# Filtered images stored in the order of the convolution's taps, and a GpSimd copy that restores the order for the queries

## The chip, the cores and the metric

The kernel runs on one core of one Trainium2 chip. The metric is the device time of one execution, in microseconds (us); lower is better.

## The reference, cut to what matters

The input x has 16 images of 64 channels and 128 x 128 pixels, in fp32. Layer 0 shifts each channel by a function of its median, upsamples by two with a 7-tap filter, applies a ReLU and downsamples. Layer 1 filters the result in the frequency domain and then runs attention in which the queries are pixels and the keys come from two strided convolutions:

```
x = layer0(x)                                   # zd in the kernel
xf = x + irfft2(rfft2(x) * gate)                # xfd: the filtered images
q = x_flat(xf) @ q_w + q_b                      # one query a pixel, 4 heads of 16
for stride in (8, 16):                          # two paths
    xs = conv(xf, sr_w, stride) + sr_b          # 64 -> 64 channels, kernel = stride
    kv = layernorm(xs) @ kv_w + kv_b            # 256 and 64 keys
    k, v = split(kv);  v = depthwise3x3(v)
out = softmax(q @ k.T / 4) @ v                  # over the 320 keys of both paths
return (out @ proj_w + proj_b) as image + x
```

## The kernel before, in words

The work has two phases. `phase1` goes over images and groups of four channels. It computes layer 0, the Fourier transform, the gate, and the inverse transform, and stores two sets of images in device memory: zd (layer 0's output) and xfd (the filtered images). The last two steps matter here. `inverse_cols` (L546) multiplies a spectrum, as the stationary operand, with the constants iv1 and iv2 (L86, L87), whose 128 columns for each of the real and imaginary parts are the positions w in an image row. `inverse_rows` (L565) finishes the transform, and GpSimd issues the store to xfd (L576), in runs of one image row of 128 elements. So the order of the columns of iv1 and iv2 is the order in which the pixels of a row lie in xfd.

`phase2` reads them twice. For the convolutions, `load_images` (L678) brings a pair of images into the tile xp: 128 partitions (two row parities x 64 channels), and in each partition 2 images x 64 rows x 128 columns. `keys_values` (from L683) is called 8 times, once for a pair of images, in the middle of the image before the pair (the first time at the start of the phase). For stride 8 it issues 32 matrix products of 512 columns, for stride 16 128 products of 128 columns (L698): each takes the 64 x 128 weights of one pair of taps (row d, column f) and, as the moving operand, every pixel that this tap meets. Two consecutive products write the two halves of the PSUM tile cp (partitions 0 to 63 and 64 to 127), so they use the two groups of 64 columns of the array. In the profile each such product is two records. L706 (VectorE) adds the bias and writes cp to xs; then come the layer norm, the keys, the values and their depthwise convolution.

For the queries, `load_part` (L786) brings one part of an image (512 pixels in each of two image halves, 128 partitions) into a tile xa with three buffers, three parts ahead; `queries` (L794) multiplies it with the query weights into qp, two parts ahead. The attention runs over blocks: 16 images x 16 parts x 2 halves = 512. The list `ORDER` (L925) fixes the order of a block's steps on TensorE: maxima of the scores (ma), scores (ss), values (av), in odd blocks the projection of the part before (pj), in even ones the queries. `ordered` (L777) keeps TensorE's and VectorE's attention instructions in this order; the rest is placed by the scheduler of the language. ScalarE takes the exponential (L862); VectorE takes the maxima (L826) and divides by the sum (L895 to L901).

The SP queue issues the loads (xp, xa, zr) and the small transfers that put the transposed maxima into the query tile (q<-nt, L835). GpSimd's queue holds in this phase the transfers of the result (L913) and, for each call of `keys_values`, four memsets of padded value tiles (L735), which wait until VectorE has read the pads of the call before.

Of the kernel before, what the change touches and what calls it, by code (L numbers as in the profile page):

```python
# [8 lines left out]
F32 = mybir.dt.float32  # L9
# [3 lines left out]
ALU = mybir.AluOpType  # L13
# [52 lines left out]
CST_AT, CST_N = _cols(_CST)  # L66
# [4 lines left out]
def _constants():  # L71

    c = np.zeros((128, CST_N), np.float64)
    i = np.arange(128)
    c[:, CST_AT["ident"]] = np.eye(128)
    c[:, CST_AT["ones"]] = 1.0
    turn = (i[:, None] * i[None, :]) % 128
    cos = np.cos(2 * np.pi * turn / 128)
    sin = np.sin(2 * np.pi * turn / 128)
    cos[turn % 64 == 32] = 0.0  # L80
    sin[turn % 64 == 0] = 0.0
    c[:, CST_AT["fh"]] = np.concatenate([cos[:, :65], -sin[:, 1:64]], 1)
    c[:, CST_AT["fwc"]] = cos / 128
    c[:, CST_AT["fws"]] = sin / 128
    c[:, CST_AT["fwn"]] = -sin / 128
    c[:, CST_AT["iv1"]] = np.concatenate([cos, sin], 1)  # L86
    c[:, CST_AT["iv2"]] = np.concatenate([-sin, cos], 1)  # L87
    fold = np.where((i == 0) | (i == 64), 1.0, 2.0)[:, None] / 128

    ihc, ihs = fold * cos, -fold * sin  # L90
    ihs[0] = ihc[64]
    c[:, CST_AT["ihc"]] = np.concatenate([ihc[:64], ihc[:64]])
    c[:, CST_AT["ihs"]] = np.concatenate([ihs[:64], ihs[:64]])
    c[:, CST_AT["rank"]] = np.arange(16)

    c[:, CST_AT["center"]] = ((i[:, None] % 64) == np.arange(C)[None, :]) - 1.0 / C

    vinit = np.zeros((128, 384), np.float32)
    for h in range(NH):
        for j in range(2):  # L100
            vinit[:, 128 * j + 32 * h + 16 : 128 * j + 32 * h + 32] = 1.0
        r, at = 64 * (h % 2), 256 + 64 * (h // 2) + 32 * (h % 2)
        vinit[r : r + 64, at + 16 : at + 32] = 1.0
    return c.astype(np.float32), vinit
# [518 lines left out]
def phase2(ctx, tc, nc, cs, ident, vinit, w2, sr1, sr2, zd, xfd, out):  # L623

    N = 512
# [4 lines left out]
    io = ctx.enter_context(tc.tile_pool(name="p2io", bufs=3))  # L630
# [23 lines left out]
    def wt(name, rows=64):  # L654
        return w2s[0:rows, W2_AT[name]]
# [27 lines left out]
    def keys_values(b, xp):  # L683

        kgs = [kvp.tile([128, NK], F32, name=f"kg{b + i}", tag="kg", bufs=3) for i in range(2)]

        vts = [ks.tile([64, NK + NK2], F32, name=f"vt{b + i}", tag=f"vt{i}") for i in range(2)]
        for s, wgt, size, cols in (("1", s1, 16, c1), ("2", s2, 8, c2)):
            stride, m = H // size, size * size
            n = f"{b}_{s}"  # L690

            c_ps = misc(f"cp{n}")
            src = xp.rearrange("p i (a d) (e f) -> p i a d e f", d=stride // 2, f=stride)
            taps = [(d, f) for d in range(stride // 2) for f in range(stride)]
            for j in range(0, len(taps), 2):
                for y in range(2):
                    d, f = taps[j + y]
                    nc.tensor.matmul(  # L698
                        c_ps[64 * y : 64 * y + 64, 0 : 2 * m],
                        wgt[:, d, f, :],  # L700
                        src[:, :, :, d, :, f],
                        start=(j == 0),
                        stop=(j + 2 == len(taps)),
                    )
            xs = ks.tile([128, 2 * m], F32, name=f"xs{n}", tag="xs")
            nc.vector.tensor_scalar(xs, c_ps[:, 0 : 2 * m], wt("srb" + s, 128), None, ALU.add)  # L706

            n_ps = misc(f"center{n}")
            nc.tensor.matmul(n_ps[0:64, 0 : 2 * m], cs("center"), xs, start=True, stop=True)
            xc = ks.tile([64, 2 * m], F32, name=f"xc{n}", tag="xc")  # L710
            nc.vector.tensor_copy(xc, n_ps[0:64, 0 : 2 * m])
            sq = ks.tile([64, 2 * m], F32, name=f"sq{n}", tag="sq")
            nc.vector.tensor_tensor(sq, xc, xc, ALU.mult)
            q_ps = misc(f"var{n}")
            nc.tensor.matmul(q_ps[0:64, 0 : 2 * m], cs("ones", 64)[:, 0:64], sq, start=True, stop=True)
            sd = ks.tile([64, 2 * m], F32, name=f"sd{n}", tag="sd")
            nc.scalar.activation(sd, q_ps[0:64, 0 : 2 * m], AF.Sqrt, scale=1.0 / C, bias=eps[0:64])
            nc.vector.reciprocal(sd, sd)
            nc.vector.tensor_tensor(xc, xc, sd, ALU.mult)
            yt = ks.tile([64, 2 * m], F32, name=f"yt{n}", tag="yt")  # L720
            nc.vector.tensor_scalar(yt, xc, wt("lng" + s), wt("lnb" + s), ALU.mult, ALU.add)


            k_ps = misc(f"kp{n}")
            nc.tensor.matmul(k_ps[:, 0 : 2 * m], wt("k" + s), yt, start=True, stop=True)
            for i in range(2):
                nc.vector.tensor_scalar(
                    kgs[i][:, cols], k_ps[:, m * i : m * i + m], wt("kb" + s, 128), D**-0.5, ALU.add, ALU.mult
                )
            v_ps = misc(f"vp{n}")  # L730
            nc.tensor.matmul(v_ps[0:64, 0 : 2 * m], wt("v" + s), yt, start=True, stop=True)
            pads = []
            for i in range(2):
                pad = ks.tile([64, size + 2, size + 2], F32, name=f"pad{n}{i}", tag=f"pad{size}", bufs=2)
                nc.gpsimd.memset(pad, 0.0)  # L735
                nc.vector.tensor_scalar(
                    pad[:, 1 : size + 1, 1 : size + 1],
                    v_ps[0:64, m * i : m * i + m].rearrange("p (a e) -> p a e", a=size),
                    wt("vb" + s),
                    None,  # L740
                    ALU.add,
                )
                pads.append(pad)
            for i in range(2):
                o = vts[i][:, cols].rearrange("p (a e) -> p a e", a=size)
                for tap in range(9):
                    src = pads[i][:, tap // 3 : tap // 3 + size, tap % 3 : tap % 3 + size]
                    w = dw[:, tap : tap + 1]
                    if tap == 0:
                        nc.vector.tensor_scalar(o, src, w, None, ALU.mult)  # L750
                    else:
                        nc.vector.scalar_tensor_tensor(o, src, w, o, ALU.mult, ALU.add)
        for i in range(2):
            vt = vts[i]
            nc.vector.tensor_copy(vt[:, NK : NK + NK2], vt[:, c2])
            t_ps = misc(f"vtp{b + i}")
            for j in range(3):
                nc.tensor.transpose(
                    t_ps[:, 64 * j : 64 * j + 64], vt[:, 128 * j : 128 * j + 128], ident[0:64, 0:64]
                )  # L760
            vb = vbs[(b + i) % 3]
            nc.scalar.copy(
                vb[:, 0:256].rearrange("p (a r) -> p a r", r=32)[:, :, 0:D],
                t_ps[:, 0:128].rearrange("p (a d) -> p a d", d=D),
            )
            for e in range(2):
                r = slice(64 * e, 64 * e + 64)
                nc.scalar.copy(
                    vb[r, 256:384].rearrange("p (a r) -> p a r", r=64)[:, :, 32 * e : 32 * e + D],
                    t_ps[r, 128:192].rearrange("p (a i d) -> p a i d", i=2, d=D)[:, :, e],  # L770
                )
            kv[b + i] = kgs[i], vb
# [12 lines left out]

    def load_part(tiles, tag, src, b, p):  # L786
        cut = slice(p * N, (p + 1) * N)
        t = io.tile([128, N], F32, name=f"{tag}{b}_{p}", tag=tag)
        v = src[b].rearrange("c (f h) w -> f c (h w)", f=2)
        for f in range(2):  # L790
            nc.sync.dma_start(out=t[64 * f : 64 * f + 64, :], in_=v[f][:, cut])
        tiles[b, p] = t

    def queries(b, p):  # L794
        xa = xas.pop((b, p))
# [133 lines left out]

    for p in range(3):  # L930
        load_part(xas, "xa", xfd, 0, p)
    for p in range(2):
        queries(0, p)
    for i in range(2):
# [4 lines left out]
    for i in range(len(blocks) + 1):  # L939
        b, p, f = blocks[i] if i < len(blocks) else (B, 0, 0)  # L940
        if f == 0 and i < len(blocks):
            if p == 0 and b % 2 == 0 and b + 2 < B:
                images = load_images(b + 2)
            if p == NP // 2 and b % 2 == 1 and b + 1 < B:
                keys_values(b + 1, xps[b + 1])
            if i + 6 < len(blocks):
                load_part(xas, "xa", xfd, *blocks[i + 6][:2])
            load_part(zrs, "zr", zd, b, p)
        next(images, None)
        this = Block(b, p, f) if i < len(blocks) else None  # L950
# [105 lines left out]
```

## Time and profile before

| | |
|---|---|
| time, median of 3 runs | 12044.02 us (12031.09 to 12055.08) |
| profiled execution's own time | 12040.97 us |
| its span | 12038.9 us |
| granted TensorE clock, mean | 0.961 |
| second phase starts at about | 5640 us |
| TensorE's convolution records (cp) | 2560, in 8 calls |
| GpSimd busy | 2181.9 us, nearly all in the first phase |

A line of the groups gives the source line, engine, operation, the tiles written and read, their shapes and the count; then the busy time in us and the mean of one in ns; then the engine's idle time before them and what ended it. L781 is a helper (`ordered`), so its rows are told apart by tile names: ss are scores, ma maxima, av values, pj the projection, qp the queries. A line of the order of time gives start and duration in us, engine, line, operation, tiles, shapes and count of records merged. PE is TensorE, PEld its weight loads, DVE VectorE, ACT ScalarE, POOL GpSimd, SPq the DMA queue of SyncE. A TensorE record's duration reaches beyond the start of the next, since products are pipelined; the distance of starts tells the rate.

### The profile page before, as it was taken

How to read it: one execution, taken by the hardware profiler on the slowest of the kernel's cores; microseconds unless marked ns; L12 is line 12 of the kernel's file. 1: busy time of each engine (PE TensorE's matmuls, PEld its weight loads, DVE VectorE, ACT ScalarE, POOL GpSimd, SP SyncE). 2: the span in 40 equal slices, each digit the busy share in tenths (PEclk: the TensorE clock that was granted, in tenths of full speed). 3: DMA queues.
4: the chain of work that ended last, by engine and by line, in shares of the span. 5: the costliest groups of instructions: out<-in, count | busy, mean ns of one | idle time of the engine just before them, and what ended most of it. 6: DMA issues, size and time to landing. Idle time of an engine off the chain costs nothing.

```text
span 12038.9 us, 192902 instructions
## 1 busy us (share of the span) xinstructions
PE 11384.5 (95%) x79360; PEld 5651.9 (47%) x79360; DVE 6008.9 (50%) x8481; ACT 5793.9 (48%) x8927; POOL 2181.9 (18%) x3366
## 2 busy tenths in 40 slices
PE   0999999999999999997999999999999999999999
PEld 0666666666666666664333333333333333333333
DVE  6777766000000000000676767757667577576777
ACT  0544545555555555553453545535445355354455
POOL 0233433333333333332000000000000000000000
PEclk9999999999999999998999999999999999999999
DMA  3222231111111111113212112121121211211111
GB/s 64 63 66 66 66 81 47 40 38 41 42 40 40 40 39 39 38 39 80 57 38 54 39 43 50 37 55 39 34 57 39 54 38 39 54 39 30 35 38 31
DMA packets 350095, 561.81 MB, mean 47 GB/s; under 512 B 82952, under 2 KB 215440, under 8 KB 346896
## 3 DMA queue, kind: packets, MB, share of 16 engines
q1 hardware_dynamic: 263184, 280.82, 10.5%
q0 software_dynamic: 86016, 268.52, 7.4%
q8 instruction: 627, 10.27, 0.4%
q14 instruction: 268, 2.20, 0.1%
HBM read 343.62 MB, written 201.33 MB: 45 GB/s over the span
## 4 chain that ended last, share of the span: by engine, by line
PE 85%; ACT 6%; POOL 2%; DMA 2%; issue 2%; DVE 1%; SPq 1%; ACTq 0%; POOLq 0%; DVEq 0%
PE av L781 13%; PE ma L781 13%; PE ss L781 12%; PE tps L393 9%; PE zps L427 6%; PE rps L365 5%; ACT e L862 4%; PE cp L698 4%; PE aps L351 4%; PE bps L546 3%; PE qp L781 2%; PE pj L781 2%; PE fps L440 2%; PE ops L565 2%; PE mps L377 1%
## 5 line engine op out<-in xcount | busy, mean ns | idle before, releaser
L862 ACT ACTIVATE e<-ss 128x1024 f32<-128x1024 f32 x2560 | 2622.2, 1024 | 2933.7 <-PE ss L781 2920.4
L781 DVE TENSOR_REDUCE nm<-ma 128x2 f32<-128x640 f32 x4096 | 3239.8, 812 | 1247.0 <-PE ss L781 805.6
L781 PE MATMUL ss<-q,kg 32*128 32x512 f32 (+1 forms) x12288 | 2837.0, 634 | 31.7 <-DMA q<-nt 31.5
L781 PE MATMUL ma<-kg,q 32*128 32x320 f32 x16384 | 2765.6, 476 | 20.6 <-DVE nm L781 19.5
L781 PEld LDWEIGHTS ma<-kg,q 32*128 32x128 f32 x16384 | 1188.4, 185 | 1542.7 <-ACT e L862 805.9
L652 DVE MEMSET eps<- 128x1 f32 x1 | 0.1, 59 | 3569.4 <-POOL sp L533 3569.4
L781 PE MATMUL av<-e,vb 128*32 128x512 f32 (+1 forms) x10240 | 1673.6, 610 | 0.0
L781 PEld LDWEIGHTS ss<-q,kg 32*128 32x128 f32 (+1 forms) x12288 | 727.3, 166 | 1296.2 <-DVE nt L781 397.6
L913 POOL DMA_DIRECT2D result<-ot x512 | 268.6, 529 | 5355.7 <-DVE ot L781 5318.6
L393 PEld LDWEIGHTS tps<-w1s,r 127*91 127x91 f32 x12288 | 1086.9, 168 | 226.2 <-ACT r L367 95.3
L393 PE MATMUL tps<-w1s,r 127*91 127x64 f32 x12288 | 1158.6, 253 | 6.3 <-ACT a L353 6.2
L351 PE MATMUL aps<-w1s,x 128*128 128x273 f32 x2048 | 598.7, 416 | 281.4 <-POOL x L341 281.4
L367 ACT ACTIVATE r<-rps 127x546 f32<-127x546 f32 x1024 | 644.5, 629 | 412.1 <-PE tps L393 380.6
L365 PE MATMUL rps<-a,w1s 64*127 64x273 f32 x4096 | 685.5, 433 | 127.3 <-ACT xf L573 106.7
L427 PE MATMUL zps<-t,w1s 91*128 91x512 f32 x1536 | 773.3, 642 | 0.4 <-ACT t L416 0.4
L180 DVE TENSOR_SCALAR_CACHE_REDUCE hit<-xm,t 128x8192 uint8<-128x8192 f32 x80 | 699.7, 8746 | 2.8
L781 PEld LDWEIGHTS av<-e,vb 128*32 128x32 f32 (+1 forms) x10240 | 266.0, 113 | 694.4 <-issue 473.4
L411 ACT COPY t<-tps 91x384 f32<-91x384 f32 x1024 | 437.1, 476 | 289.5 <-PE tps L403 192.2
L351 PEld LDWEIGHTS aps<-w1s,x 128*128 128x128 f32 x2048 | 360.7, 193 | 418.4 <-POOL x L341 281.4
L365 PEld LDWEIGHTS rps<-a,w1s 64*127 64x127 f32 x4096 | 361.5, 190 | 412.0 <-ACT xf L573 196.1
L353 ACT COPY a<-aps 128x546 f32<-128x546 f32 x512 | 314.3, 614 | 435.8 <-PE aps L351 432.5
L546 PE MATMUL bps<-csb,sp 128*64 128x256 f32 x4096 | 516.1, 396 | 4.5 <-POOL sp L535 4.5
(149 smaller groups left out, 11475.8 us busy)
## 6 DMA issues: line engine op xcount, KB each, us to landing
x<-x POOLq DMA_DIRECT2D x256, 256.0 KB, 3.6
xm<-x SPq DMA_DIRECT2D x32, 2048.0 KB
zd<-z POOLq DMA_DIRECT2D x256, 256.0 KB, 2.7
xfd<-xf POOLq DMA_DIRECT2D x256, 256.0 KB, 2.8
xp<-xfd SPq DMA_DIRECT2D x128, 512.0 KB
xa<-xfd SPq DMA_DIRECT2D x512, 128.0 KB
zr<-zd SPq DMA_DIRECT2D x512, 128.0 KB
result<-ot POOLq DMA_DIRECT2D x512, 128.0 KB, 2.9
```

Of the source, the lines that this page charges most:

```text
L180: nc.vector.tensor_scalar(hit, xm[f], thr, None, op, ALU.add, accum_out=cnt)
L351: nc.tensor.matmul(a_ps[:, i, 0:UPT], x4s[b, g][:, 2 * p + i, :], ut, start=True, stop=True)
L353: nc.scalar.copy(a, a_ps[:, :, 0:UPT])
L365: nc.tensor.matmul(r_ps[0:WING, k, 0:UPT], uw[half], a[half, i, :], start=True, stop=True)
L367: nc.scalar.activation(r, r_ps[0:WING, :, 0:UPT], AF.Relu, scale=4.0)
L393: nc.tensor.matmul(t_ps[0:UPN, i, at : at + 64], r[i][:, k, UPN * j : UPN * j + UPN], dw[0:WING, k, :], start=True, stop=True,)
L411: nc.scalar.copy(t4[:, :, 2 * p + i, :], t_ps[0:UPN, i, 0:384].rearrange("p (j w) -> p j w", j=3))
L427: nc.tensor.matmul(z_ps, dtp[0:UPN, j, :], t4[:, j].rearrange("p g w -> p (g w)"), start=(j == 0), stop=(j == 2))
L546: nc.tensor.matmul(b_ps[64 * i : 64 * i + 64, 256 * q : 256 * q + 256], s[:, r, 2 * q + i, 0:64], cs("iv2" if r else "iv1"), start=(r == 0 ...
L698: nc.tensor.matmul(c_ps[64 * y : 64 * y + 64, 0 : 2 * m], wgt[:, d, f, :], src[:, :, :, d, :, f], start=(j == 0), stop=(j + 2 == len(taps)),)
L781: last[engine] = op(*args, **kw).ins
L862: nc.scalar.activation(e, s_ps, AF.Exp)
```

## The change

The columns of iv1 and iv2 are permuted, so that a row of a filtered image is stored as 16 runs of eight: position 8f + e holds the pixel 16e + f. The pixels that a tap of stride 16 meets in a row (fixed f, all e) are then eight neighbours; those of a tap of stride 8 are two runs of eight, h = 0 and 1, in which e' = 2e + h. The convolution's moving operand is read accordingly, and L706 puts the columns of xs back in order while it adds the bias (for stride 16 there is one run, and nothing to put back).

The queries need the pixels in their own order, since zr and the result have it. So each loaded part is copied by GpSimd (`own_order`) from xa into a new tile xo in pixel order; xa has two buffers instead of three, xo has two, and `queries` reads xo.

```
-    c[:, CST_AT["iv1"]] = np.concatenate([cos, sin], 1)
-    c[:, CST_AT["iv2"]] = np.concatenate([-sin, cos], 1)
+    turned = i.reshape(8, 16).T.reshape(128)
+    c[:, CST_AT["iv1"]] = np.concatenate([cos, sin], 1)[:, np.concatenate([turned, 128 + turned])]
+    c[:, CST_AT["iv2"]] = np.concatenate([-sin, cos], 1)[:, np.concatenate([turned, 128 + turned])]
...
-            src = xp.rearrange("p i (a d) (e f) -> p i a d e f", d=stride // 2, f=stride)
+            parts = 16 // stride
+            src = xp.rearrange("p i (a d) (h f e) -> p (i a) d h f e", d=stride // 2, h=parts, f=stride)
...
-                        src[:, :, :, d, :, f],
+                        src[:, :, d, :, f, :],
...
-            nc.vector.tensor_scalar(xs, c_ps[:, 0 : 2 * m], wt("srb" + s, 128), None, ALU.add)
+            nc.vector.tensor_scalar(
+                xs.rearrange("p (a e h) -> p a h e", e=8, h=parts),
+                c_ps[:, 0 : 2 * m].rearrange("p (a h e) -> p a h e", e=8, h=parts),
+                wt("srb" + s, 128), None, ALU.add,
+            )
...
-        t = io.tile([128, N], F32, name=f"{tag}{b}_{p}", tag=tag)
+        t = io.tile([128, N], F32, name=f"{tag}{b}_{p}", tag=tag, bufs=2 if tag == "xa" else None)
...
+    def own_order(b, p):
+
+        xo = io.tile([128, N], F32, name=f"xo{b}_{p}", tag="xo", bufs=2)
+        nc.gpsimd.tensor_copy(
+            xo.rearrange("p (a e f) -> p a f e", e=8, f=16),
+            xas[b, p].rearrange("p (a f e) -> p a f e", e=8, f=16),
+        )
+        xas[b, p] = xo
...
     for p in range(3):
         load_part(xas, "xa", xfd, 0, p)
+        own_order(0, p)
...
             if i + 6 < len(blocks):
                 load_part(xas, "xa", xfd, *blocks[i + 6][:2])
+                own_order(*blocks[i + 6][:2])
```

## The prediction

> **What bounds the kernel now.** I read the page's busy times and the chain that ended last first.
>
> ```profile
> PE 11384.5 (95%) x79360; PEld 5651.9 (47%) x79360; DVE 6008.9 (50%) x8481; ACT 5793.9 (48%) x8927; POOL 2181.9 (18%) x3366
> PE 85%; ACT 6%; POOL 2%; DMA 2%; issue 2%; DVE 1%; SPq 1%; ACTq 0%; POOLq 0%; DVEq 0%
> PE av L781 13%; PE ma L781 13%; PE ss L781 12%; PE tps L393 9%; PE zps L427 6%; PE rps L365 5%; ACT e L862 4%; PE cp L698 4%; PE aps L351 4%; PE bps L546 3%; PE qp L781 2%; PE pj L781 2%; PE fps L440 2%; PE ops L565 2%; PE mps L377 1%
> ```
>
> TensorE sets the end, and the convolution (cp) has 4% of the chain, near 480 us. Next, the groups of the second phase, shapes apart, for cp and for pj, a product on the same 128 rows and two groups of 64 columns:
>
> ```profile
> L781 PE MATMUL pj<-on,w2s 128*64 128x512 f32 x1024 | 283.5, 630 | 5.8 <-ACT vb L768 4.4 <-DVE on L781 1.5
> L698 PE MATMUL cp<-xp,s 128*64 128x512 f32 x512 | 236.7, 1098 | 47.0 <-DMA xa<-xfd 47.0
> L698 PE MATMUL cp<-xp,s 128*64 128x128 f32 x2048 | 233.3, 405 | 1.1 <-DVE pad L736 1.1
> ```
>
> Same size, but 1098 ns against 630. Then TensorE's order of time, around the second pair of images and, last two lines, in the first phase:
>
> ```profile
> 6312.65 29.58 PE L698 MATMUL cp<-xp,s 128*64 128x512 f32 x64
> 6342.17 1.13 PE L781 MATMUL ss<-q,kg 32*128 32x512 f32 x4
> ...
> 6364.99 29.52 PE L698 MATMUL cp<-xp,s 128*64 128x128 f32 x256
> ...
> 3033.27 1.95 PE L546 MATMUL bps<-csb,sp 128*64 128x256 f32 x16
> ...
> 3039.83 1.14 PE L440 MATMUL fps<-csb,z 128*128 128x128 f32 x8
> ```
>
> Records stand in pairs, one for each column group, which start together. cp with 512 columns: 32 pairs in 29.4 us, 0.92 us a pair, 1.79 ns a column. cp with 128: 128 pairs, 0.23 us each, again 1.8 ns a column. bps, the same geometry with contiguous input and also accumulating: less its last duration of 0.38 us, 7 steps in 1.57 us, 0.22 us for 256 columns, 0.87 ns a column (the first step is the long one; the rest take 0.216). So a column costs cp twice as much, whether its input steps by 32 bytes (stride 8) or 64 (stride 16). Nothing else runs on TensorE meanwhile, and the groups that touch cp say who waits:
>
> ```profile
>   DVE xs L706: 507.2, 16
> ```
>
> Lastly, the start of the first cp, which follows a long idle time:
>
> ```profile
> 5691.94 0.24 PEld L698 LDWEIGHTS cp<-xp,s 128*64 128x64 f32 x2 [0.68 <-issue]
> 5692.86 0.19 PEld L698 LDWEIGHTS cp<-xp,s 128*64 128x64 f32 x2 [0.68 <-issue]
> ```
>
> The weight load gets faster as the clock rises, but the step stays 0.92 us: cp is limited by the reading of its input, not by the array.
>
> **What the Trainium skill says.** "SBUF — State Buffer", Specifications (TRN2): SBUF has lines of 16 bytes, and full bandwidth needs at least two hits on a line. Before, each fp32 element lies in another line; afterwards eight neighbours fill two lines. The trace agrees with the penalty (1.8 against 0.87 ns a column); runs of eight occur nowhere in it. "GPSIMD Engine Reference", section 7, prices loops at 1.9 cycles an element, 2.9 where the read steps over 8 bytes; no strided copy is in the trace. "SBUF — State Buffer", Who interferes with whom: a GpSimd instruction that reads SBUF and a VectorE instruction with two SBUF inputs exclude each other for their whole length; the trace has nothing on it. "TensorE: Matmul & The Clock Gate", Part 1: an idle TensorE falls to half its clock and needs some 3.4 us of work to leave it; this agrees: the stretch 6365 to 6394 has a granted clock of 0.94, so 29 x 0.06 / 0.5 = 3.5 us at half speed.
>
> **The change, part by part.**
>
> First phase: columns of two constants are permuted. Shapes, counts and transfers are the same: 0 us. The stored images are as large and written in the same runs: 0.
>
> cp, 512 columns (8 times, once for each pair of images): I take the contiguous column, 0.436 us a pair (512 x 0.85, from bps' 0.216 for 256). 32 x 0.436 = 13.95 instead of 29.4: 15.4 us saved. The first, starting cold, runs its first 4 us at half clock, where a contiguous pair takes 0.87: 5 pairs at 0.87 and 27 at 0.436 are 16.1, 13.4 saved. Sum 7 x 15.4 + 13.4 = 121 us.
>
> cp, 128 columns (8 times): nearest row is fps, 128 columns with 128 weight columns, 8 records in 1.14 us, less 0.36 for the last, 7 steps, 0.112 each; a pair here also loads 2 x 64 weight columns. At half clock a step is 0.222, hardly faster than the strided one: 3.5 us do 16 pairs, the other 112 take 12.5 us, together 16.0 instead of 29.4: 13.4 saved, 8 times 107 us.
>
> Bounds of both: above, ideal reading with no slow start, 2 x (29.4 - 13.9) x 8 = 248. Below: if the first two elements of each run of eight cost the strided price, a column costs (2 x 1.8 + 6 x 0.85) / 8 = 1.09 ns, which gives back (32 x 0.12 + 112 x 0.03) x 8 = 58. If loading of weights and issue bound the short ones at 0.16 us a pair, 112 x 0.05 x 8 = 45 more. If a run helps nothing, the gain is 0.
>
> Nothing takes the gain: during the long cp VectorE and ScalarE wait, and during the short one VectorE's work on the first half's values ends at 6370.6 (the memset that waits for it starts there), 6 us into it, well before 16.
>
> xs (L706): the long one writes every second element, 0.75 us now; between +0 and +0.75, I take +0.3: 8 x 0.3 = 2.
>
> GpSimd's 256 copies: nearest row
>
> ```profile
> L341 POOL TENSOR_TENSOR x<-x,sb 128x512 f32<-128x512 f32 x256 | 274.5, 1072 | 1156.0 <-DMA x<-x 879.4 <-DMA sb<-row 276.6
> ```
>
> 1.07 us for as many elements with two inputs; the skill's 2.9 cycles would give 1.24 us. I take 1.3, bounds 0.8 and 3. They run on an idle engine: in steady state GpSimd issues two result transfers per 21.7 us. A copy waits for its transfer and for the query product two parts before (two buffers of xo), so it runs right after one query product and is used by the second after it, two parts (43 us) later. Queued behind it are result transfers, which nobody waits for within a part. TensorE's order is the same in both programs, the query products included; also VectorE's and ScalarE's.
>
> The SP queue keeps its order but for part loads, which run one part further ahead. The load of part k waited for the query product of k-3; now it waits for the copy of k-2, which the product of k-4 releases. At one place in the queue, where the load of the next part now stands, the same product releases it, one copy, 1.3 us, later. Behind it stand rows of maxima (q<-nt), a block early in steady state: hidden. After each pair's convolution, image loads stand there too, and TensorE already waits at 6452.73 for a q<-nt behind them (4.8 us; 31.5 in six such waits). 1.3 us later in each of 7: 9 us; bounds -30 (waits gone) and +20.
>
> At the same place GpSimd's queue holds the memsets of the next pads, which wait for VectorE until 6411. Before them stands part 12's copy, behind them part 13's; it waits for the query product at 6427.43 in any case, and the one that needs it ran at 6479.15: some 50 us of cover. Without it each us late would be a us lost, 7 times.
>
> Sum: 121 + 107 - 2 - 9 = 217. The profiled run took 12040.97 us (span 12038.9, 2 us around it), 3 below the median of 12044.02. 12041 - 217 = 11824, on the median's footing 11827; I say 11826.
>
> **Rivals.** (a) Reading in runs of eight is only partly cured, or weights bound the short products: 58 to 103 less gain, 11,885 to 11,930. For it: no such run in the trace. Against: the line rule, and fps. (b) The change doesn't do what it says: the reading stays at 1.8 ns a column for another reason than the step. Then 12041 + 11 = 12,052, same within error. Against: bps has everything else in common. (c) Slower: the copy excludes VectorE. VectorE's only two-input instruction in a steady block with a copy is the multiplication by the reciprocal sums:
>
> ```profile
> 6782.96 1.13 PE L781 MATMUL qp<-xa,w2s 64*128 64x512 f32 x4
> ...
> 6790.67 0.41 DVE L781 TENSOR_TENSOR at<-at,rd 128x256 f32<-128x256 f32 x1
> ```
>
> The copy can start at 6784.1, so up to 6.5 us it touches nothing. VectorE has about 1 us of slack there (idle 0.28 and 0.84 before its next waits); each further us stops the maxima and so TensorE, 256 times. The gain of 217 is gone at 6.5 + 1 + 0.85 = 8.4 us; at 9 us the time is 11826 + 1.5 x 256 = 12,210. Against: the price above is a sixth of it.
>
> **How the numbers follow.** Full reading rate 0.70 (11,795 to 11,860), (a) 0.18, (b) 0.06, (c) 0.06. A difference of 0.2% (24 us, as wide as the runs before lie apart) is about what can be told from no change. Faster 0.88, same 0.06, slower 0.06. The range reaches from the ideal reading with the waits for q<-nt gone (12044 - 248 - 20, near 11,780) to the end of (a): 11,780 to 11,930.
>
> **What would show it.** cp's records at about 0.6 us (512) and 0.3 (128), spans of 14 and 16 us a pair of images instead of 29.5 twice; the wait of xs for cp near 280 us instead of 507; GpSimd's copies at 1 to 2 us after qp; no TensorE idle time released by a copy; steady blocks still 10.85 us. It would be wrong if cp stays above 20 us a piece, if copies take over 6 us, or if blocks lengthen.

## The result, and the profile after

| | before | after |
|---|---|---|
| median of 4 runs | 12049.55 us | 11850.12 us |
| lowest and highest | 12031.09 to 12057.37 | 11835.04 to 11853.21 |
| profiled execution's own time | 12040.97 | 11835.04 |
| its span | 12038.9 | 11833.3 |
| time after over time before | | 0.9834, 95% interval 0.9817 to 0.9851 |

The kernel is faster by 199 us; the time lies 24 us above the forecast of 11826 and inside its range. First the page of the changed kernel: busy times, and the chain that ended last.

```profile
PE 11163.2 (94%) x79360; PEld 5609.8 (47%) x79360; DVE 6015.8 (51%) x8481; ACT 5788.3 (49%) x8927; POOL 2452.9 (21%) x3622
PE 85%; ACT 6%; POOL 2%; issue 2%; DMA 2%; DVE 1%; SPq 0%; ACTq 0%; POOLq 0%; DVEq 0%
PE av L789 13%; PE ma L789 13%; PE ss L789 12%; PE tps L395 9%; PE zps L429 6%; PE rps L367 5%; ACT e L879 4%; PE aps L353 4%; PE bps L548 4%; PE qp L789 3%; PE pj L789 2%; PE cp L702 2%; PE fps L442 2%; PE ops L567 2%; PE mps L379 1%
```

TensorE is busy for 221 us less (11384.5 before), GpSimd for 271 us more, which is its 256 copies; VectorE and ScalarE are as they were. The convolution (cp) has half of its former share of the chain, 2% instead of 4%. TensorE still sets the end.

Next the groups of the second phase, different shapes apart; columns are the busy time in us, the mean of one in ns, and the idle time ahead of it with what ended it.

```profile
L789 PE MATMUL qp<-xo,w2s 64*128 64x512 f32 x1024 | 303.4, 648 | 56.8 <-ACT e L879 56.8
L789 PE MATMUL pj<-on,w2s 128*64 128x512 f32 x1024 | 283.5, 631 | 5.8 <-ACT vb L776 4.3 <-DVE on L789 1.5
L805 POOL COPY xo<-xa 128x512 f32<-128x512 f32 x256 | 272.0, 1063 | 2528.4 <-issue 2344.5 <-PE qp L789 136.8 <-DMA xa<-xfd 47.1
L702 PE MATMUL cp<-xp,s 128*64 128x128 f32 x2048 | 129.0, 294 | 1.1 <-DVE pad L744 1.1
L702 PE MATMUL cp<-xp,s 128*64 128x512 f32 x512 | 113.1, 600 | 47.9 <-DMA xa<-xfd 47.9
```

The convolution's two lines carry the gain: 236.7 + 233.3 = 470.0 us before, 113.1 + 129.0 = 242.1 now, 227.9 saved. With 512 columns a record takes 600 ns, no more than the contiguous product pj of the same size (631). The query product (qp) carries a loss: its own time is the same, but TensorE stands idle ahead of it for 56.8 us in all, against 35.2 before, and the view puts this down to ScalarE's exponentials (e). The same group before the change, and a line of the view of waits before the change (us in all, times, longest):

```profile
L781 PE MATMUL qp<-xa,w2s 64*128 64x512 f32 x1024 | 303.5, 655 | 35.2
PEld qp L781 <- ACT e L862: 177.3, 240, 0.7
```

So the exponential, which frees the PSUM tile of the query product, ended the wait of 240 of the 256 products before the change too; but the line of the products notes no releaser there, where the single idle times are as short as 0.147 us. VectorE's wait for the convolution answers as well; this is the line of the groups that touch cp:

```profile
  DVE xs L710: 280.0, 16
```

It was 507.2. Then TensorE's order of time around the second pair of images, and two query products some 250 us later (start, duration, and in brackets the idle time ahead with its releaser):

```profile
6278.73 13.95 PE L702 MATMUL cp<-xp,s 128*64 128x512 f32 x64
6292.61 1.13 PE L789 MATMUL ss<-q,kg 32*128 32x512 f32 x4
...
6315.98 15.45 PE L702 MATMUL cp<-xp,s 128*64 128x128 f32 x256
...
6610.72 1.13 PE L789 MATMUL qp<-xo,w2s 64*128 64x512 f32 x4 [0.24 <-ACT e L879]
6632.50 1.13 PE L789 MATMUL qp<-xo,w2s 64*128 64x512 f32 x4 [0.24 <-ACT e L879]
```

The two convolutions take 13.95 and 15.45 us instead of 29.58 and 29.52. The two query products are one part apart: 21.78 us. The same two of the kernel before, in the same view:

```profile
6609.36 1.13 PE L781 MATMUL qp<-xa,w2s 64*128 64x512 f32 x4
6631.06 1.13 PE L781 MATMUL qp<-xa,w2s 64*128 64x512 f32 x4
```

21.70 us, with no idle time long enough to be noted. Over all parts of both traces the median distance goes from 21.70 to 21.79, and the median idle time ahead of a query product from 0.147 to 0.237 us. GpSimd, meanwhile, is far from late; its own order of time in the changed kernel:

```profile
6298.71 1.06 POOL L805 COPY xo<-xa 128x512 f32<-128x512 f32 x1 [26.43 <-issue]
6321.54 0.76 POOL L743 MEMSET pad<- 64x324 f32 x2 [21.77 <-DVE vt L760]
6348.55 0.37 POOL L743 MEMSET pad<- 64x100 f32 x2 [26.25 <-DVE vt L760]
6355.68 1.04 POOL L930 DMA_DIRECT2D result<-ot  x2 [6.76 <-DVE nm L789]
6365.51 1.06 POOL L805 COPY xo<-xa 128x512 f32<-128x512 f32 x1 [8.79 <-issue]
```

A copy runs as soon as a query product has freed its buffer, and is read two parts later. So the question for the experiments was: what holds a query product back by 0.09 us, 240 times (21.6 us by the sums of idle time), if the copy is not late, and ScalarE does the same work as before?

### The profile page after: what moved, and what is told of

Same layout as the page of the kernel before. It is cut to its first block, busy times and chain, and to the rows that moved or that the text cites. A ratio compares the mean times of both kernels' runs of the same rounds, so it can differ in the third digit from the quotient of the medians.

```text
span 11833.3 us, 193897 instructions
## 1 busy us (share of the span) xinstructions
PE 11163.2 (94%) x79360; PEld 5609.8 (47%) x79360; DVE 6015.8 (51%) x8481; ACT 5788.3 (49%) x8927; POOL 2452.9 (21%) x3622
## 4 chain that ended last, share of the span: by engine, by line
PE 85%; ACT 6%; POOL 2%; issue 2%; DMA 2%; DVE 1%; SPq 0%; ACTq 0%; POOLq 0%; DVEq 0%
PE av L789 13%; PE ma L789 13%; PE ss L789 12%; PE tps L395 9%; PE zps L429 6%; PE rps L367 5%; ACT e L879 4%; PE aps L353 4%; PE bps L548 4%; PE qp L789 3%; PE pj L789 2%; PE cp L702 2%; PE fps L442 2%; PE ops L567 2%; PE mps L379 1%
## 5 line engine op out<-in xcount | busy, mean ns | idle before, releaser
L789 PE MATMUL ss<-q,kg 32*128 32x512 f32 (+1 forms) x12288 | 2845.3, 635 | 31.1 <-DMA q<-nt 30.5
L789 PE MATMUL ma<-kg,q 32*128 32x320 f32 x16384 | 2767.9, 476 | 21.0 <-DVE nm L789 19.5
L805 POOL COPY xo<-xa 128x512 f32<-128x512 f32 x256 | 272.0, 1063 | 2528.4 <-issue 2344.5
L434 POOL DMA_DIRECT2D zd<-z x256 | 198.2, 774 | 1672.8 <-ACT z L433 1671.3
```

The lines of the kernel that those rows point to most:

```text
L789: last[engine] = op(*args, **kw).ins
L805: nc.gpsimd.tensor_copy(xo.rearrange("p (a e f) -> p a f e", e=8, f=16), xas[b, p].rearrange("p (a f e) -> p a f e", e=8, f=16),)
```

## The experiments

Three theories stood against each other. W: a wait. Before the change, the query product waits for one engine, ScalarE, which frees its PSUM tile; the transfer of its part had long landed. Afterwards it waits for two, ScalarE and GpSimd, as the order of instructions with their waits shows, and the second wait costs time even when what it waits for is long done. P: the copies, by running, disturb another engine. R: the new order of the data itself costs something. The "phase 2" column counts from the convolution's first record to the end of the span, which leaves out the first phase, whose length differs by some us between profiles of any kernel. "Idle" is the median idle time of TensorE ahead of a query product.

| kernel | median us | ratio to before, 95% | phase 2, us | part, us | idle, us |
|---|---|---|---|---|---|
| before | 12049.55 | 1 | 6350.6 | 21.70 | 0.147 |
| after | 11850.12 | 0.9834, 0.9817 to 0.9851 | 6152.5 | 21.79 | 0.237 |
| e1: order set where q is written | 11894.52 | 0.9869, 0.9854 to 0.9884 | 6193.5 | 21.97 | 0.147 |
| e2: copy alone, added to before | 12071.06 | 1.0016, 1.0009 to 1.0023 | 6371.6 | 21.79 | 0.238 |
| e3: copy added, nobody reads it | 12047.97 | 0.9995, 0.9989 to 1.0002 | 6352.7 | 21.70 | 0.146 |
| e4: copy on ScalarE | 11822.64 | 0.9817, 0.9804 to 0.9830 | 6130.4 | 21.70 | 0.146 |
| e5: order set at q, written in neighbours | 11829.64 | 0.9817, 0.9804 to 0.9831 | 6130.0 | 21.70 | 0.146 |
| e6: runs of 2 pixels | 11833.23, one run | | 6140.7 | 21.70 | 0.146 |
| e7: runs of 4 pixels | 11832.28, one run | | 6130.2 | 21.70 | 0.146 |

The first four experiments ran on one chip, with 12051.59 us as the median of before; the last three on another, with 12053.76.

**The copy without the new order (e2).** On the kernel before: the same copy at the same places with the same buffers, but each value keeps its place in the part. The copy still goes through the values in the tap order, so it now steps by 64 bytes in its reading as well as in its writing. Images and convolution stay as they were.

```diff
-        t = io.tile([128, N], F32, name=f"{tag}{b}_{p}", tag=tag)
+        t = io.tile([128, N], F32, name=f"{tag}{b}_{p}", tag=tag, bufs=2 if tag == "xa" else None)
...
+    def own_order(b, p):
+        xo = io.tile([128, N], F32, name=f"xo{b}_{p}", tag="xo", bufs=2)
+        nc.gpsimd.tensor_copy(
+            xo.rearrange("p (a e f) -> p a f e", e=8, f=16),
+            xas[b, p].rearrange("p (a e f) -> p a f e", e=8, f=16),
+        )
+        xas[b, p] = xo
...
+        own_order(0, p)
...
+                own_order(*blocks[i + 6][:2])
```

> The kernel before, with GpSimd's copy alone: each part is copied from xa to xo in unchanged order, and the query product reads xo; constants and convolution are those of before. Theory W: 23 us slower than before, near 12,073, parts at 21.79 us, the product's idle time 0.24 us. Rival R: as before, 12,050, parts at 21.70. If the strided writing of the copy mattered, this copy without it would cost less than 23.

Measured: slower than before by 0.16%, 19.5 us by the medians, and 21.0 us in phase 2. The groups of its second phase:

```profile
L781 PE MATMUL qp<-xo,w2s 64*128 64x512 f32 x1024 | 303.3, 647 | 57.1 <-ACT e L871 57.1
L797 POOL COPY xo<-xa 128x512 f32<-128x512 f32 x256 | 271.8, 1062 | 2652.1 <-issue 2454.1 <-PE qp L781 150.8 <-DMA xa<-xfd 47.2
```

The idle time ahead of the query product is that of the changed kernel (57.1 and 56.8 us), with the convolution and the order of all data as before. So R falls for this loss. The copy took 1062 ns with steps of 64 bytes on both sides, and 1063 ns in the changed kernel, which reads neighbours: stepping in the reading, beside a stepped writing, cost GpSimd nothing. What stepping in the writing costs is not shown, since every copy of the study does it, this one too, against the last sentence of the expectation.

**The copy that nobody reads (e3).** On the kernel before: the copy of e2, with steps of 64 bytes on both sides, but its result goes nowhere, and the query product reads the loaded part as before.

```diff
+    def own_order(b, p):
+        xo = io.tile([128, N], F32, name=f"xo{b}_{p}", tag="xo", bufs=1)
+        nc.gpsimd.tensor_copy(
+            xo.rearrange("p (a e f) -> p a f e", e=8, f=16),
+            xas[b, p].rearrange("p (a e f) -> p a f e", e=8, f=16),
+        )
...
+        own_order(0, p)
...
+                own_order(*blocks[i + 6][:2])
```

> The kernel before, with the same copies by GpSimd, but nobody reads xo (one buffer), and the query product reads xa. GpSimd's work and its use of SBUF stay, the wait of the query product on GpSimd goes. Theory W: same as before, 12,050 within 0.1%, parts 21.70. Rival P (the copies disturb other engines, as by excluding VectorE): 23 us slower, parts 21.79.

Measured: no difference from before that can be told, and phase 2 within 2 us. The groups:

```profile
L781 PE MATMUL qp<-xa,w2s 64*128 64x512 f32 x1024 | 303.4, 654 | 35.1
L797 POOL COPY xo<-xa 128x512 f32<-128x512 f32 x256 | 268.8, 1050 | 3518.9 <-DMA xa<-xfd 3518.7
```

All 256 copies run and take 1.05 us each, and the idle time ahead of qp is 35.1 us, as before (35.2). These copies cost the other engines nothing. They start when their part has landed (the releaser named is the transfer), not after a query product as in e2, so the time of the copy differs too; but in the changed kernel and in e2 the last copy ahead of a query product had ended 19.4 us before its weight load (median), and the next starts only after the product. P falls. What e2 has and e3 has not is that TensorE waits for the copy.

**The copy on the engine that TensorE waits for anyway (e4).** One word of the changed kernel:

```diff
-        nc.gpsimd.tensor_copy(
+        nc.scalar.copy(
```

> The changed kernel with its copies on ScalarE, the engine for which the query product waits anyway. Theory W: one wait again, the product's idle time at 0.15 us; but ScalarE gets 256 copies of some 0.7 us. If these fit its idle time: near 11,827. If they delay the exponentials by as much as they last: up to 11,827 + 180. Rival R or P (any copy costs it, wherever it waits): the product's idle time stays at 0.24 us.

Measured: 11822.64 us, and phase 2 is 22.0 us shorter than in the changed kernel. The groups:

```profile
L789 PE MATMUL qp<-xo,w2s 64*128 64x512 f32 x1024 | 303.5, 655 | 37.4 <-ACT e L879 3.4
L805 ACT COPY xo<-xa 128x512 f32<-128x512 f32 x256 | 269.7, 1054 | 62.3 <-DMA xa<-xfd 48.1 <-PE qp L789 14.2
```

The same work, done on an engine busy for half of the span, and the idle time is gone. The two waits of the query product, for its PSUM tile and for its input, are now for one engine.

How the second wait takes its time can be read in the trace's records on TensorE's queue. Before, in e3 and in e4, the first weight load of the query product carries the wait for ScalarE itself; in 240 of the 256 products it starts 42 to 43 ns after ScalarE has signalled the end of its exponential. In the changed kernel and in e2 a semaphore instruction of 51 ns stands ahead of it and carries the wait for ScalarE, while the weight load carries the one for GpSimd. The semaphore instruction starts 28 ns after ScalarE's signal, the weight load 76 ns after that, and the record of the product another 31 ns later, where it was 2 ns before. From the signal to the product these are 0.135 us instead of 0.043. So ScalarE ends the wait in both kernels, and what the second wait does is to lengthen the way from ScalarE's signal to the product by 0.09 us, though GpSimd's last copy had ended 19.4 us before. In this form W is shown. What a second wait costs where both engines have long been done is not shown.

Two counts keep this from being read too widely. A semaphore instruction as such did not cost: e1 and e5 have some 250 more of them than before (2007 against 1760, as many as the changed kernel's 2013), but about 243 of these stand ahead of maxima (ma) whose weight load waits for nothing itself and starts 4 ns after them, and e5's parts are as short as before. And the pair of waits is not peculiar to GpSimd: in each of these traces it stands ahead of 9 weight loads of the keys (kp), which wait for VectorE and ScalarE, again some 76 ns apart; what it costs there was not measured.

**No copy at all (e1).** On the changed kernel: own_order and its calls are left out, the parts have three buffers again, and ScalarE, which adds the bias to the query product and writes q, puts the values in their new places. The edit of that instruction:

```diff
-            nc.scalar.activation(q, q_ps[:, f, :], AF.Identity, bias=qb)
+            nc.scalar.activation(
+                q.rearrange("p (a e f) -> p a f e", e=8, f=16),
+                q_ps[:, f, :].rearrange("p (a f e) -> p a f e", e=8, f=16),
+                AF.Identity, bias=qb,
+            )
```

> The new storage order and the convolution's new reading stay; the copies go, and ScalarE puts the pixels back in order while it writes the query tile (L802 of before), which it does anyway. Theory W (the copies cost 0.09 us a part, because the query product now waits for two semaphores, one of which needs an instruction of its own ahead of the weight load): the product's TensorE idle time goes from 0.24 back to 0.15 us, a part from 21.79 back to 21.70 us, and the time is 256 x 0.09 = 23 us below the changed kernel, near 11,827; cp stays at 14.1 and 16.1 us a call. Rival R (the 0.09 us come from the new order itself, not from the copies): parts stay at 21.79 and the time at 11,850. If ScalarE's strided write is slow, its 512 instructions take over 0.69 us each and parts get longer.

Measured: 11894.52 us, 44 us slower than the changed kernel by the medians, where W expected a gain. W's sign for the wait was right (the idle time is 0.147 us again), but parts are longer, 21.97 us. The groups show why; first ScalarE's writing of q, then the query product:

```profile
L810 ACT ACTIVATE q<-qp,w2s 128x512 f32<-128x512 f32 x512 | 512.9, 1098 | 119.3 <-PE qp L789 118.0 <-DMA q<-nt 1.2 <-DMA xp<-xfd 0.2
L789 PE MATMUL qp<-xa,w2s 64*128 64x512 f32 x1024 | 303.2, 654 | 35.2
```

The activation takes 1098 ns, where the kernel before has 684: twice 0.41 us for each part, on the way from the query product to the scores, of which 0.27 reach the end. TensorE's score products (ss) waited for q for 0.2 us in all before; here they do so for 87.8 us. ScalarE's line before the change:

```profile
L802 ACT ACTIVATE q<-qp,w2s 128x512 f32<-128x512 f32 x512 | 324.1, 684 | 133.3 <-PE qp L781 132.1 <-DMA q<-nt 1.0 <-DMA xp<-xfd 0.2
```

Two theories for it. S: ScalarE is slow where it writes to SBUF with a step of 64 bytes. T: it is the reordering as such, reading in PSUM included, that costs.

**The same with neighbours written (e5).** Only the order in which the activation goes through the same values: it reads PSUM with a step of eight values and writes neighbours.

```diff
             nc.scalar.activation(
-                q.rearrange("p (a e f) -> p a f e", e=8, f=16),
-                q_ps[:, f, :].rearrange("p (a f e) -> p a f e", e=8, f=16),
+                q.rearrange("p (a e f) -> p a e f", e=8, f=16),
+                q_ps[:, f, :].rearrange("p (a f e) -> p a e f", e=8, f=16),
```

> No copies; ScalarE restores the order at the query tile as in the first experiment, but the other way round: it reads PSUM with a step of 8 elements and writes SBUF in neighbours, where the first read neighbours and wrote with a step of 16 elements (64 bytes), at 1102 ns an instruction instead of 684. Theory S (the 64-byte step of the write costs ScalarE the 0.42 us, and that delays TensorE by 0.27 us a part): about 684 to 720 ns, parts 21.70 us, time as with the copies on ScalarE, 11,822, or lower by what ScalarE no longer copies. Rival T (any order but the straight one costs ScalarE that much, read or written): 1100 ns, parts 21.97, time 11,895.

Measured: 11829.64 us, phase 2 as in e4. The groups:

```profile
L810 ACT ACTIVATE q<-qp,w2s 128x512 f32<-128x512 f32 x512 | 323.7, 683 | 119.9 <-PE qp L789 118.2 <-DMA q<-nt 1.3 <-DMA xp<-xfd 0.4
L789 PE MATMUL qp<-xa,w2s 64*128 64x512 f32 x1024 | 303.1, 654 | 35.1
L702 PE MATMUL cp<-xp,s 128*64 128x128 f32 x2048 | 127.6, 292 | 1.1 <-DVE pad L744 1.1
L702 PE MATMUL cp<-xp,s 128*64 128x512 f32 x512 | 113.7, 602 | 47.6 <-DMA xa<-xfd 47.6
```

683 ns, as with no reordering. S holds and T falls; e4's copy, which ScalarE also wrote with steps of 64 bytes, had taken 1054 ns. The convolution is as fast as in the changed kernel, the idle time as small as before the change, and no engine does any work more than before. With e4 it is the best version of the study; each has a ratio of 0.9817, and both spans' second phases are some 22 us shorter than that of the changed kernel. The medians of e4 and e5 can't be told apart.

**How many neighbours does the reading need? (e6, e7)** On the kernel before, the storage unchanged: each product of the convolution takes runs of 2 (e6) or 4 (e7) neighbouring pixels in place of single ones; shapes, counts and everything else stay. The weights of a tap thus meet pixels of other taps: both kernels leave out the right choice of pixels, and only their times are of use. Each ran once; compared are the durations of its 16 convolutions. The edit of e6 (e7 has e=4):

```diff
-            src = xp.rearrange("p i (a d) (e f) -> p i a d e f", d=stride // 2, f=stride)
+            src = xp.rearrange("p i (a d) (h f e) -> p (i a) d h f e", d=stride // 2, f=stride, e=2)
...
-                        src[:, :, :, d, :, f],
+                        src[:, :, d, :, f, :],
```

> The kernel before, storage unchanged, where the convolution alone reads in runs of 2 neighbours (so the taps meet wrong pixels, and the output is not the reference's); no copies. Line theory (two hits on a line of 16 bytes give the full rate): 14.1 and 16.1 us a call as with runs of eight, 228 us less than before. Rival (each run's start costs 0.9 ns, whatever its length): a column costs (1.79 + 0.84) / 2 = 1.3 ns, 21 and 23 us a call, near 11,940.

> As the run before, but with runs of 4 neighbours (one line of 16 bytes each); the output is not the reference's. Line theory: 14.1 and 16.1 us a call. Rival (each run's start costs 0.9 ns): 1.08 ns a column, 17.7 and 19.6 us a call, some 170 us less than before.

Measured, groups of e6:

```profile
L698 PE MATMUL cp<-xp,s 128*64 128x128 f32 x2048 | 142.0, 306 | 1.1 <-DVE pad L736 1.1
L698 PE MATMUL cp<-xp,s 128*64 128x512 f32 x512 | 116.4, 610 | 48.4 <-DMA xa<-xfd 48.4
```

And of e7:

```profile
L698 PE MATMUL cp<-xp,s 128*64 128x128 f32 x2048 | 127.4, 292 | 1.1 <-DVE pad L736 1.1
L698 PE MATMUL cp<-xp,s 128*64 128x512 f32 x512 | 113.8, 603 | 47.9 <-DMA xa<-xfd 47.9
```

For a pair of images the two convolutions take 29.6 and 29.2 us with single pixels, 14.55 and 17.75 with runs of 2, 14.2 and 15.9 with runs of 4, 14.1 and 16.1 with runs of eight. Nearly all of the gain is there with two neighbours, that is 8 bytes, and all of it with four. This is what "SBUF — State Buffer", Specifications (TRN2), in the Trainium skill states of its lines of 16 bytes (at least two hits on a line for full bandwidth), and the runs agree, but for the products of 128 columns, where runs of 2 still cost some 1.7 us a call. The rival of the expectations, a price for the start of each run, would have given 21 and 23 us with runs of 2 and 17.7 and 19.6 with runs of 4; it falls.

## Why the prediction was right, and where it was not

**The convolution: right.** The prediction took 13.95 us for a call of 512 columns, 16.1 for the first of them, and 16.0 for one of 128, and 228 us saved in all. Measured: 13.95, 15.4 for the first, and 16.1 on average, 227.9 saved in the two groups, and VectorE's wait went from 507.2 to the expected 280. That a contiguous product of the same geometry in the first phase gives the price of the repaired one, and that a start at half clock must be added, both held: in the four short convolutions looked at, the granted clock of their 16 us was 0.87 to 0.92. Rival (a), a partial cure, and (b), none, are excluded by those durations; with e6 and e7 the cause of the old price is also shown, not only argued: it goes with the number of neighbours in a run.

**"No TensorE idle time released by a copy", "steady blocks still 10.85 us": wrong.** This is the step that failed. Blocks are 10.895 us (half of 21.79), and the price is 21.6 us by the idle time ahead of the query products (56.8 against 35.2). The prediction asked whether a copy would be late and counted the cover, two parts, and for that e3 shows it right: the work is hidden. But it put the price of a second wait that is already satisfied at nothing, without a reason. The copy is what puts a new engine among those that the query product waits for, and the prediction followed only what is queued behind the copy on GpSimd, not what the wait itself is on TensorE's queue, between ScalarE's signal and the product. e2 shows the loss alone (+21.0 us in phase 2), e4 takes it away alone (-22.0).

**The copy's price: right in kind.** 1.3 us taken, 1.06 measured. The prediction's figure from the Trainium skill ("GPSIMD Engine Reference", section 7) gave 1.24 us for it, which is over the measured value too; the nearest row of the trace (1.07) was the better source. That figure is for stepped reading, moreover, and the copy reads neighbours and steps in its writing; for reading without steps the same section has 1.9 cycles, an estimate of 0.81 us for this copy. The measured copies agree with neither, and are as long with stepped reading (e2, 1062 ns) as without. Rival (c) needed copies of over 8.4 us and is excluded; VectorE's multiplication by the reciprocal sums, which it would have stopped, took 409 ns and 407 before. As for the exclusion of GpSimd and VectorE, no copy ran long enough here to show it.

**xs +2 us: 0.** The group's durations are 350 to 753 ns, before 349 to 751. Writing every second element cost VectorE nothing.

**Waits for q<-nt +9 us: -1.** They went from 31.5 to 30.5 us in all, on TensorE's score products. That part loads run one part further ahead did not show.

**The cover of the memsets: held.** They still wait for VectorE and no query product waits for a copy behind them.

**The sum.** The prediction summed to 217. With the measured sizes of its own terms it would have been 227.9 - 0 + 1, about 229; less 22 for the wait that it put at nothing, about 207. The profiled spans differ by 205.6, which looks like agreement, but 7.5 of that lies ahead of the convolution's first record (at 5688.24 and 5680.79 us), in the first phase, where nothing changed but the order of columns in two constants: this much is luck. Phase 2 itself is 198.1 us shorter. So some 8 us of the convolution's gain do not arrive. e5, which has no copy and no second wait, shows the same: 220.6 us shorter with 228.7 saved in the convolution; e7 too, 220.4 with 228.8. The loss therefore belongs neither to the copy nor to the wait. It may come with the shorter convolution, about 1 us for each of its 8 calls, but in e6, with 211.6 saved, 209.9 arrive. The granted clock of the 66 us after the short convolution was 0.79 to 0.82, against 0.79 to 0.87 before; this could be it, but no run tells it apart, and it stays open.

## What to carry to other kernels

Where a matrix product is slower than its columns, look at the step of its moving operand: two to four fp32 neighbours in each run brought it to the price of contiguous reading here. The cheapest place to undo the new order was an instruction that runs anyway, ScalarE's move of the query product from PSUM to SBUF, provided that it wrote neighbours and took the step on its PSUM side. When work is moved to an idle engine, ask for whom the bounding engine now waits: here a second engine in a wait that already held TensorE up cost it 0.09 us each time, although its data had long been there, while the same work on the engine that it waited for already was free. And a releaser named in a view of waits need not be later than before for the wait to grow: ScalarE ended this wait in both kernels, and what had grown was the time from its signal to the product. Take away the reader, or move the producer, to find out.

## What the runs showed of the hardware that was not expected

- A query product that waits for ScalarE and GpSimd instead of ScalarE alone starts 0.09 us later after ScalarE's signal (0.135 instead of 0.043 us), with GpSimd's last copy ended 19.4 us before: 21 to 22 us over 240 of them. A semaphore instruction of 51 ns, which carries the wait for ScalarE, stands 76 ns ahead of the weight load, which carries the other.
- ScalarE took 1098 instead of 684 ns for 512 values a partition when it wrote them to SBUF with steps of 64 bytes. Reading them from PSUM with steps of 32 bytes and writing neighbours took 683.
- GpSimd's copy of as many values took 1063 ns with the step of 64 bytes in its writing alone, and 1062 with it in its reading too. VectorE, writing every second value, was no slower either (753 and 751 ns).
- Runs of two fp32 neighbours were enough for the convolution with 512 columns (14.55 us against 29.6 with single values and 14.1 with eight), and nearly so with 128 (17.75 against 29.2 and 16.1).
